# First eight taps of a per-position convolution as three products of 12-bit parts, with a scaling in PSUM

## The chip, the cores and the metric

The kernel runs on one core of a Trainium2 chip. The time is device time of one execution in microseconds (us), from the first instruction to the last, as the median of several runs. The engines that matter are TensorE (PE; its weight loads are listed apart as PEld), VectorE (DVE), ScalarE (ACT), GpSimd (POOL) and the queue that issues transfers (SP).

## What is computed

A network of four layers on x, an array of 4 images x 32 x 32 positions x 16 channels. Three layers are convolutions with weights of their own for every output position (i, j); one (the interval layer, third in order) is another small computation that shares the core. Cut to what matters, a convolution layer with M, W of 1024 x 1024 and G of 1024 x 3 x 3 x 16 x 16 is

```python
def layer(inputs, M, W, G):                       # inputs: the normalised x, (b, h, w, c)
    first = einsum('ijyx,byxc->bijc', M, inputs)
    kern = G -> (h*w*f, c, 3, 3)                  # 16 filters f for each of the 1024 output positions
    shifted = conv(inputs, kern, 'SAME')          # (b, ij, f, y, x)
    diff = relu(inputs[:, None, None] - shifted)  # (b, ij, y, x, f)
    second = einsum('ijyx,bijyxc->bijc', W, diff)
    return first - second
x = x + layer(group_norm(x), M, W, G)
```

The bulk is `shifted`: for every image, filter and output position a picture of 32 x 32, of which only a weighted sum (with W) of its clipped difference is kept. All inputs are float32.

## The kernel before

Images are worked on in two groups g of two; a phase is one group in one layer, in the order (0, layer), (1, layer) for three layers, six in all. In a phase, 8 chunks of 128 output positions are taken in turn, and in a chunk 16 filters x 2 images, so that there are 6 x 8 x 32 = 1536 steps. A step makes one PSUM tile of 128 output positions x 1024 points of the picture. The contraction is over 16 channels x 9 taps: the points' neighbourhoods lie in `im` as two halves of 64 partitions (one for the upper, one for the lower half of the picture), each with four taps x 16 channels in slots 0 and 1 (eight taps), and the ninth tap in slot 2. The two halves are separate matmuls on separate rows of TensorE, each into one bank of PSUM.

Slots 0 and 1 are plain float32 matmuls. The ninth tap goes as one matmul in the one-pass type float32r: slot 2 holds the same 16 channels four times, and `halve` with `halve_rest` changes some of the copies so that the four products are those of the high and low parts of the two factors.

VectorE then takes the minimum of the sum with 0, multiplies it with W and sums it up, in one instruction of 1024 elements per step (identity is subtracted from the weights in `prep`, so that the difference comes out of the matmul).

```python
    def halve(dst, src, mask):
        nc.scalar.activation(dst, src, AF.Copy, scale=mask[:, 1:2])

    def halve_rest(dst, src, mask):
        nc.vector.scalar_tensor_tensor(
            dst, src, mask[:, 0:1], dst.bitcast(F32), op0=ALU.mult, op1=ALU.add
        )

    def prep(u, at=0, to=FU):

        if u >= n_chunks * NU:
            return
        if at == 0:
            units[u] = (raws.pop(u), wpool.tile([P, FU, P], F32R, tag="W9", name=f"W9_{u}"))
        raw, W9 = units[u]
        f0 = u % NU * FU
        nc.gpsimd.tensor_tensor(
            raw[:, 1, at:to], raw[:, 1, at:to],
            pick[:, f0 + at : f0 + to].unsqueeze(2).to_broadcast([P, to - at, P]),
            ALU.subtract,
        )
        halve(W9[:, at:to], raw[:, 2, at:to], low_w)

    def prep_rest(u, at=0, to=FU):
        if u in units:
            raw, W9 = units[u]
            halve_rest(W9[:, at:to], raw[:, 2, at:to], low_w)
```

(cut: group norm, transposition, transfers of the neighbourhoods). The first term is a set of float32 matmuls for each group and layer, placed among the steps of a phase:

```python
    def first_term(g, layer):

        xn = xns[g]
        ps = bank(f"pf_{g}{layer}")
        for half in range(2):
            mt = wpool.tile([P, NT // 2, 4, 256], F32, tag="MT", bufs=1, name=f"MT_{g}{layer}{half}")
            nc.sync.dma_start(mt, convs[layer][0][half])
            yield 12
            for k in range(NT // 2):
                pt = NT // 2 * half + k
                for j in range(4):
                    nc.tensor.matmul(
                        ps[32 * j : 32 * j + 32, :256], lhsT=xn[:, pt, :], rhs=mt[:, k, j, :],
                        start=pt == 0, stop=pt == NT - 1, tile_position=(0, 32 * j),
                    )
        yield 2
        ft = work.tile([P, NT * GC], F32, tag="fs", name=f"ft_{g}{layer}")
        nc.vector.transpose(ft, ps[:, : NT * GC])
        yield 1
        nc.vector.tensor_tensor(
            X[g], X[g], ft.rearrange("p (t m) -> p t m", t=NT), ALU.add
        )
        yield 1
```

(cut: the interval layer, except for its inner loop.)

```python
        def step(name, ftp, rt, bias):

            ft = ivp.tile([P, QI, T1], F32, tag="ft", name=f"ft_{name}{g}")
            nc.scalar.copy(ft, ftp)
            yield 2
            s = ivp.tile([P, QI, T1], F32, tag="s", name=f"s_{name}{g}")
            last = None
            for i in range(QI + 1):
                if i < QI:
                    t = ivp.tile([P, T1, T1], F32, tag="dp", bufs=2, name=f"dp_{name}{g}{i}")
                    nc.gpsimd.tensor_tensor(
                        t,
                        ft[:, i, :].unsqueeze(1).to_broadcast([P, T1, T1]),
                        rt,
                        ALU.add,
                    )
                if last is not None:
                    nc.vector.tensor_reduce(s[:, i - 1, :], last, axis=AX.X, op=ALU.max)
                last = t
                yield 3
            for q in range(NQ):
                o = slice(GC * q, GC * (q + 1))
                nc.scalar.activation(
                    r[R:, QI * q : QI * (q + 1), :], s[o], AF.Sigmoid, bias=bias[o]
                )
            yield 2
```

The work of the next phase is a generator, `behind`: at each step's end the program resumes it if the number of steps that it last yielded have gone by. Every engine executes its instructions in the order in which the program issues them.

```python
    def conv_layer(phase, behind):

        g, layer = phases[phase]
        wait = 0
        imv = im[g].rearrange("p s b (y x) -> p s b y x", x=HP)
        im9v = im9[g].rearrange("p b (y x) -> p b y x", x=HP)
        acc = work.tile([P, NT, GC], F32, tag="acc", bufs=2, name=f"acc_{phase}")
        for t in range(NT):
            n = phase * NT + t
            steps = [(f, b) for f in range(C) for b in range(GB)]
            if n == 0:
                steps.sort(key=lambda s: (s[0] // FU, s[1]))
            for at, (f, b) in enumerate(steps):
                u = n * NU + f // FU
                if at % (FU * GB) == 2:
                    load_raw(u + 3)
                if at % (FU * GB) == (8 if u == 0 else 2):
                    prep(u + 1)
                if at % (FU * GB) == (12 if u == 0 else 8):
                    prep_rest(u + 1)
                if at == 4:
                    load_chunk(n + 1)
                W, W9 = units[u]

                ps = bank_pair(f"pc_{n}_{f}_{b}")
                for slot in range(3):
                    for h in range(2):
                        r = slice(64 * h, 64 * h + 64)
                        w, v = (W9[r], im9v[r, b]) if slot == 2 else (W[r, slot], imv[r, slot, b])
                        nc.tensor.matmul(
                            ps[:, h, :],
                            lhsT=w[:, f % FU, :],
                            rhs=v[:, :, :H],
                            start=slot == 0,
                            stop=slot == 2,
                        )

                col = b * C + f
                junk = work.tile([P, NP], F32, tag="junk", name=f"junk_{n}_{col}")
                nc.vector.scalar_tensor_tensor(
                    junk,
                    ps.rearrange("p h n -> p (h n)"),
                    0.0,
                    chunks[n],
                    op0=ALU.min,
                    op1=ALU.mult,
                    accum_out=acc[:, t, col : col + 1],
                )
                wait -= 1
                if wait <= 0:
                    wait = next(behind, 1 << 20)
            nc.vector.tensor_tensor(X[g][:, t], X[g][:, t], acc[:, t], ALU.add)
        for _ in behind:
            pass
```

The start of the program normalises the first two images itself; `normal` for the second image runs on GpSimd (three operations of 128 x 542).

## Time and profile before

| | |
|---|---|
| time, median of 3 runs | 3073.79 us (3072.03 to 3076.02) |
| span of the profiled execution | 3074.8 us |
| granted clock of TensorE | 0.999 |
| ScalarE busy | 145.8 us |
| GpSimd busy | 305.4 us |
| data moved | 215.20 MB, mean 70 GB/s |
| WT, raw: landing after issue | 6.5 us each |
| PE `pf`, line 251, x384 | 23.2 us |
| GpSimd subtraction of 128 x 1024 (line 149), mean | 1878 ns |

A row of the page's list of groups reads: line of the program, engine, operation, output<-inputs, shapes, count | busy us, mean ns of one | idle time of the engine ahead of them and what ended most of it. Busy time of PE contains the modelled tail of every matmul, so that 99% doesn't say that the array works at its peak; the distance between the starts of instructions does. The timeline has a start in us, a length in us, the engine, line, operation and count.

### The profile page before, as it was taken

What the parts mean: (1) busy time and instruction counts of PE and PEld (TensorE: products, weight loads), DVE (VectorE), ACT (ScalarE), POOL (GpSimd) and SP (SyncE); (2) the same over time, 40 slices, a digit from 0 to 9 for tenths busy, and PEclk for the clock granted to TensorE, in tenths of its full rate; (3) what the DMA queues carried; (4) which work ended last, traced back from release to release, by engine and by line L of the source; (5) the groups of instructions that cost most, each with busy time, mean ns of one, the idle gap of its engine ahead of it and who ended that gap; (6) DMA issues with size and microseconds to landing.
All of it is one profiled execution on the core that took longest, in us unless ns stands there. A gap on an engine that the chain in (4) does not pass through costs nothing.

```text
span 3074.8 us, 38073 instructions
## 1 busy us (share of the span) xinstructions
PE 3058.7 (99%) x15826; PEld 1951.4 (63%) x15826; DVE 2125.4 (69%) x3397; ACT 145.8 (5%) x156; POOL 305.4 (10%) x201
## 2 busy tenths in 40 slices
PE   8999999999999999999999999999999999999999
PEld 4555876557765556875555544685654578677776
DVE  7766666766666666666678876668877666666666
ACT  1000000000000000000000100000000000000000
POOL 3100000100000000000013310001331000000000
PEclk9999999999999999999999999999999999999999
DMA  3331112321111232111121113211113211121100
GB/s 146 125 127 67 55 49 76 102 93 48 62 62 48 72 124 76 49 63 55 48 76 49 62 63 119 76 48 53 65 48 127 76 48 71 48 76 49 69 28 2
DMA packets 36429, 215.20 MB, mean 70 GB/s; under 512 B 10400, under 2 KB 11424, under 8 KB 22560
## 3 DMA queue, kind: packets, MB, share of 16 engines
q1 hardware_dynamic: 29696, 207.65, 18.5%
q10 hardware_dynamic: 6432, 5.10, 0.8%
q8 instruction: 124, 2.03, 0.3%
q14 instruction: 49, 0.40, 0.0%
q0 software_dynamic: 128, 0.02, 0.0%
HBM read 211.77 MB, written 0.98 MB: 69 GB/s over the span
## 4 chain that ended last, share of the span: by engine, by line
PE 99%; DVE 0%; issue 0%; DMA 0%; SPq 0%; DVEq 0%
PE pc L461 98%; PE pf L251 1%; DVE junk L471 0%; DMA im<-in_xi 0%; PE ps_l L353 0%; DVE pp L315 0%; PE ps_r L369 0%; PE ps_y L422 0%; DVE im L593 0%; DVE im L601 0%; SPq L73 0%; DVE X L483 0%; DVE W L125 0%; DVEq L601 0%
## 5 line engine op out<-in xcount | busy, mean ns | idle before, releaser
L461 PE MATMUL pc<-im,raw 64*128 64x512 f32 x12288 | 2990.7, 590 | 5.4 <-DVE junk L471 3.5
L471 DVE SCALAR_TENSOR_TENSOR junk<-pc,WT 128x1024 f32<-128x1024 f32 x1536 | 1879.7, 1224 | 940.4 <-PE pc L461 934.7
L461 PEld LDWEIGHTS pc<-im,raw 64*128 64x128 f32 x12288 | 1635.8, 186 | 754.6 <-issue 461.2
L461 PE MATMUL pc<-im,W 64*128 64x512 f32 x3072 | 1636.2, 806 | 0.0
L461 PEld LDWEIGHTS pc<-im,W 64*128 64x128 f32 x3072 | 470.0, 186 | 336.4 <-issue 288.4
L149 POOL TENSOR_TENSOR raw<-raw,pick 128x1024 f32<-128x1024 f32 (+1 forms) x97 | 182.1, 1878 | 1923.9 <-DMA raw<-in_g 1824.9
L122 ACT ACTIVATE W<-raw,low_w 128x1024 fp32r<-128x1024 f32 (+1 forms) x97 | 110.6, 1141 | 2469.6 <-PE pc L461 2468.3
L125 DVE SCALAR_TENSOR_TENSOR W<-raw,low_w,W 128x1024 fp32r<-128x1024 f32 (+1 forms) x97 | 138.0, 1423 | 0.0
L471 DVE DVE_READ_ACCUMULATOR junk<-pc,WT 128x1 f32 x1536 | 127.5, 83 | 0.0
L389 POOL TENSOR_TENSOR dp_a<-ft_a,rt_r 128x1089 f32<-128x1089 f32 x16 | 39.1, 2450 | 73.2 <-DVE s_a L396 49.4
L389 POOL TENSOR_TENSOR dp_b<-ft_b,rt_r 128x1089 f32<-128x1089 f32 x16 | 37.2, 2330 | 90.1 <-DVE s_b L396 46.6
L251 PE MATMUL pf<-MT,xn 128*32 128x256 f32 x384 | 23.2, 382 | 0.0
L181 POOL PARTITION_ALL_REDUCE sum_mc<-part_mc x6 | 2.7, 445 | 190.4 <-DVE part_mc L174 184.4
L396 DVE TENSOR_REDUCE s_b<-dp_b 128x33 f32<-128x1089 f32 x16 | 20.5, 1283 | 0.0
L396 DVE TENSOR_REDUCE s_a<-dp_a 128x33 f32<-128x1089 f32 x16 | 20.5, 1282 | 0.0
L251 PEld LDWEIGHTS pf<-MT,xn 128*32 128x32 f32 x384 | 11.2, 109 | 13.1 <-issue 6.9
L483 DVE TENSOR_TENSOR X<-X,acc 128x32 f32<-128x32 f32 x48 | 11.8, 247 | 1.5
L122 ACT ACTIVATE im<-im,low_x 128x1088 fp32r<-128x1088 f32 (+1 forms) x7 | 7.5, 1073 | 110.6 <-DMA im<-xs 106.2
L181 POOL PARTITION_ALL_REDUCE sum_mi<-part_mi x2 | 0.9, 446 | 116.1 <-DVE part_mi L174 116.1
L335 DVE TENSOR_TENSOR pp<-pp 64x1024 f32<-64x1024 f32 x10 | 12.1, 1213 | 0.0
L330 DVE TENSOR_TENSOR pp<-pp 64x1024 f32<-64x1024 f32 x10 | 12.1, 1212 | 0.0
L181 POOL PARTITION_ALL_REDUCE sum_vc<-part_vc x6 | 2.6, 442 | 89.2 <-DVE part_vc L174 83.3
(96 smaller groups left out, 140.7 us busy)
## 6 DMA issues: line engine op xcount, KB each, us to landing
raw<-in_g SPq DMA_DIRECT2D x95, 1536.0 KB, 6.5
WT<-in_w SPq DMA_DIRECT2D x48, 512.0 KB, 6.5
MT<-in_mt SPq DMA_DIRECT2D x12, 2048.0 KB, 7.8
im<-xs ACTq DMA_DIRECT2D x60, 67.8 KB, 3.1
im<-xs SPq DMA_DIRECT2D x60, 67.8 KB, 3.0
im<-in_xi SPq DMA_DIRECT2D x2, 816.0 KB, 9.2
raw<-in_g SPq DMA_DIRECT2D x1, 1152.0 KB, 9.8
raw<-in_g ACTq DMA_DIRECT2D x1, 384.0 KB, 4.2
```

The costliest lines, as they stand in the source:

```text
L122: nc.scalar.activation(dst, src, AF.Copy, scale=mask[:, 1:2])
L125: nc.vector.scalar_tensor_tensor(dst, src, mask[:, 0:1], dst.bitcast(F32), op0=ALU.mult, op1=ALU.add)
L149: nc.gpsimd.tensor_tensor(raw[:, 1, at:to], raw[:, 1, at:to], pick[:, f0 + at : f0 + to].unsqueeze(2).to_broadcast([P, to - at, P]), ALU.s ...
L181: nc.gpsimd.partition_all_reduce(m, part, channels=P, reduce_op=bass_isa.ReduceOp.add)
L251: nc.tensor.matmul(ps[32 * j : 32 * j + 32, :256], lhsT=xn[:, pt, :], rhs=mt[:, k, j, :], start=pt == 0, stop=pt == NT - 1, tile_position= ...
L330: nc.vector.tensor_tensor(pp[k][:, :H, M:], a[:, :H, M:], a[:, s : H + s, M:], ALU.max)
L335: nc.vector.tensor_tensor(pp[k][:, :H, M:], a[:, :H, M:], a[:, :H, M - s : M - s + H], ALU.max)
L389: nc.gpsimd.tensor_tensor(t, ft[:, i, :].unsqueeze(1).to_broadcast([P, T1, T1]), rt, ALU.add,)
L396: nc.vector.tensor_reduce(s[:, i - 1, :], last, axis=AX.X, op=ALU.max)
L461: nc.tensor.matmul(ps[:, h, :], lhsT=w[:, f % FU, :], rhs=v[:, :, :H], start=slot == 0, stop=slot == 2,)
L471: nc.vector.scalar_tensor_tensor(junk, ps.rearrange("p h n -> p (h n)"), 0.0, chunks[n], op0=ALU.min, op1=ALU.mult, accum_out=acc[:, t, co ...
L483: nc.vector.tensor_tensor(X[g][:, t], X[g][:, t], acc[:, t], ALU.add)
```

## The change

The eight taps of slots 0 and 1 are computed from one-pass float32r matmuls. Both factors are cut into an upper part (the bits that a mask with `HIGH` leaves, 12 fewer than float32) and the lower rest; w = wu + wl and v = vu + vl. Instead of the four products wu vu, wu vl, wl vu, wl vl, the kernel forms three, with e = 2^-12:

- WU x iy = wu vu and WL x iz = wl (vl / e), summed in PSUM;
- ScalarE multiplies this sum in PSUM, in place, with 1 + e;
- WD x iyz = (wl - e wu)(vu - vl / e) is added to it by TensorE, together with the ninth tap.

Worked out, (1 + e)(wu vu + wl vl / e) + (wl - e wu)(vu - vl / e) is wu vu + wl vl / e + e wu vu + wl vl + wl vu - wl vl / e - e wu vu + wu vl, which is the whole product. The purpose is fewer passes of TensorE over the same contraction. For it

- each unit of weights now has tiles WU, WL, WD (two slots each) and W9, made by one masking on VectorE, two scalings on ScalarE, and a copy, two operations of 1024 elements and two of 512 (on 32 partitions each) on GpSimd; a unit is 4 filters instead of 8, so there are 192 units of 8 steps;
- the neighbourhoods get tiles iy, iz, iyz;
- a step has two parts: `first_part` (8 matmuls, then the scaling), and `second_part` (6 matmuls, then the sum), which is issued after the first part of the next step;
- PSUM is four pairs of banks for everything (before: three pairs and two single banks);
- the first terms of both groups are computed together, once per layer, so M is read once per layer; MT shares a buffer with the tables of the interval layer; the inner loop of that layer yields 6 steps instead of 3.

The core of the diff (cut: the start's other reorderings, buffers of the interval layer, names):

```diff
-FU = 8
+FU = 4
 NU = C // FU
 BIG = 1.0e9
+EPS = 2.0**-12
+HIGH = -(1 << 12)
 T1 = H + 1
 NQ = 4
 QI = H // NQ
...
+    def upper(src, name):
+
+        t = work.tile([P, 2, PITCH], F32, tag="upper", bufs=2, name=f"upper_{name}")
+        t = t.rearrange("p s n -> p (s n)")[:, : src.shape[1] * src.shape[2]]
+        t = t.rearrange("p (s n) -> p s n", s=src.shape[1])
+        nc.vector.tensor_scalar(
+            t.bitcast(I32), src.bitcast(I32), HIGH, None, op0=ALU.bitwise_and
+        )
+        return t
+
+    def prep(u, at=0, to=FU, eng=nc.gpsimd):
+
+        if u >= n_chunks * NU:
+            return
+        f0 = u % NU * FU
+        eng.tensor_tensor(
+            raws[u][:, 1, at:to], raws[u][:, 1, at:to],
+            pick[:, f0 + at : f0 + to].unsqueeze(2).to_broadcast([P, to - at, P]),
+            ALU.subtract,
+        )
+
+    def prep_rest(u, at=0, to=FU, eng=nc.gpsimd):
 
         if u >= n_chunks * NU:
             return
         if at == 0:
-            units[u] = (raws.pop(u), wpool.tile([P, FU, P], F32R, tag="W9", name=f"W9_{u}"))
-        raw, W9 = units[u]
-        f0 = u % NU * FU
-        nc.gpsimd.tensor_tensor(
-            raw[:, 1, at:to], raw[:, 1, at:to],
-            pick[:, f0 + at : f0 + to].unsqueeze(2).to_broadcast([P, to - at, P]),
-            ALU.subtract,
-        )
-        halve(W9[:, at:to], raw[:, 2, at:to], low_w)
-
-    def prep_rest(u, at=0, to=FU):
-        if u in units:
-            raw, W9 = units[u]
-            halve_rest(W9[:, at:to], raw[:, 2, at:to], low_w)
+            units[u] = [
+                wpool.tile([P, 2, FU, P], F32R, tag=tag, name=f"{tag}_{u}")
+                for tag in ("WU", "WL", "WD")
+            ] + [wpool.tile([P, FU, P], F32R, tag="W9", name=f"W9_{u}")]
+        src = raws[u]
+        if to == FU:
+            del raws[u]
+        w8 = src[:, :2, at:to].rearrange("p s f k -> p s (f k)")
+        w9 = src[:, 2, at:to]
+        WU, WL, WD = (t[:, :, at:to].rearrange("p s f k -> p s (f k)") for t in units[u][:3])
+        W9 = units[u][3][:, at:to]
+        high = upper(w8, f"w{u}{at}")
+        nc.scalar.activation(WD, high, AF.Copy, scale=-EPS)
+        halve(W9, w9, low_w)
+        eng.tensor_copy(WU, high)
+        eng.tensor_tensor(WL, w8, high, ALU.subtract)
+        for r in (slice(32, 64), slice(96, 128)):
+            eng.tensor_tensor(W9[r], W9.bitcast(F32)[r], w9[r], ALU.add)
+        eng.tensor_tensor(WD, WD.bitcast(F32), WL.bitcast(F32), ALU.add)
+
+    def split(eng, g, b, name):
+        high = upper(raw[:, :2, b], f"x{name}{b}")
+        eng.tensor_copy(iy[g][:, :, b], high)
+        eng.tensor_tensor(iz[g][:, :, b], raw[:, :2, b], high, ALU.subtract)
...
-                yield 3
+                yield 6
...
+    def products(ps, pairs, first):
+        for k, (w, v) in enumerate(pairs):
+            for h in range(2):
+                r = slice(64 * h, 64 * h + 64)
+                nc.tensor.matmul(
+                    ps[:, h, :],
+                    lhsT=w[r],
+                    rhs=v.rearrange("p (y x) -> p y x", x=HP)[r, :, :H],
+                    start=first and k == 0,
+                    stop=k == len(pairs) - 1,
+                    skip_group_check=not first,
+                )
+
+    def first_part(step):
+        phase, t, f, b = step
+        g = phases[phase][0]
+        n = phase * NT + t
+        WU, WL, WD, W9 = (w[..., f % FU, :] for w in units[n * NU + f // FU])
+        ps = bank_pair(f"pc_{n}_{f}_{b}")
+        products(
+            ps,
+            [(WU[:, s], iy[g][:, s, b]) for s in range(2)]
+            + [(WL[:, s], iz[g][:, s, b]) for s in range(2)],
+            True,
+        )
+        nc.scalar.activation(ps, ps, AF.Copy, scale=1.0 + EPS)
+        return ps
+
+    def second_part(step, ps):
+
+        phase, t, f, b = step
+        g = phases[phase][0]
+        n = phase * NT + t
+        WU, WL, WD, W9 = (w[..., f % FU, :] for w in units[n * NU + f // FU])
+        products(
+            ps, [(WD[:, s], iyz[g][:, s, b]) for s in range(2)] + [(W9, im9[g][:, b])], False
+        )
+        col = b * C + f
+        junk = work.tile([P, NP], F32, tag="junk", name=f"junk_{n}_{col}")
+        nc.vector.scalar_tensor_tensor(
+            junk,
+            ps.rearrange("p h n -> p (h n)"),
+            0.0,
+            chunks[n],
+            op0=ALU.min,
+            op1=ALU.mult,
+            accum_out=accs[phase][:, t, col : col + 1],
+        )
+        if (f, b) == (C - 1, GB - 1):
+            nc.vector.tensor_tensor(X[g][:, t], X[g][:, t], accs[phase][:, t], ALU.add)
+
+    accs = {}
+    open_steps = []
+
     def conv_layer(phase, behind):
 
-        g, layer = phases[phase]
+
...
-                if at % (FU * GB) == 2:
+                if at % (FU * GB) == 1:
+                    prep_rest(u + 1)
+                    prep(u + 2)
                     load_raw(u + 3)
-                if at % (FU * GB) == (8 if u == 0 else 2):
-                    prep(u + 1)
-                if at % (FU * GB) == (12 if u == 0 else 8):
-                    prep_rest(u + 1)
                 if at == 4:
                     load_chunk(n + 1)
-                W, W9 = units[u]
-
-
-                ps = bank_pair(f"pc_{n}_{f}_{b}")
-                for slot in range(3):
-                    for h in range(2):
-                        r = slice(64 * h, 64 * h + 64)
-                        w, v = (W9[r], im9v[r, b]) if slot == 2 else (W[r, slot], imv[r, slot, b])
-                        nc.tensor.matmul(
-                            ps[:, h, :],
-                            lhsT=w[:, f % FU, :],
-                            rhs=v[:, :, :H],
-                            start=slot == 0,
-                            stop=slot == 2,
-                        )
-
-                col = b * C + f
-                junk = work.tile([P, NP], F32, tag="junk", name=f"junk_{n}_{col}")
-                nc.vector.scalar_tensor_tensor(
-                    junk,
-                    ps.rearrange("p h n -> p (h n)"),
-                    0.0,
-                    chunks[n],
-                    op0=ALU.min,
-                    op1=ALU.mult,
-                    accum_out=acc[:, t, col : col + 1],
-                )
+                step = (phase, t, f, b)
+                open_steps.append((step, first_part(step)))
+                if len(open_steps) > 1:
+                    second_part(*open_steps.pop(0))
...
         def rest_of_start():
-        prep_rest(0, F0, FU)
-        for slot in (2, 0, 1):
+        for slot in (0, 1, 2):
             normal(nc.gpsimd, 1, slot)
             sides(nc.gpsimd, 1, slot)
-        yield 4
-        halve(im9[0][:, 1], im[0][:, 2, 1], low_x)
         yield 1
```

## The prediction

> **What bounds the kernel now.** I read the page from the top: busy time by engine, then the chain that ended last, then the costliest groups.

> ```profile
> PE 3058.7 (99%) x15826; PEld 1951.4 (63%) x15826; DVE 2125.4 (69%) x3397; ACT 145.8 (5%) x156; POOL 305.4 (10%) x201
> PE pc L461 98%; PE pf L251 1%; DVE junk L471 0%; DMA im<-in_xi 0%; PE ps_l L353 0%; DVE pp L315 0%; PE ps_r L369 0%; PE ps_y L422 0%; DVE im L593 0%; DVE im L601 0%; SPq L73 0%; DVE X L483 0%; DVE W L125 0%; DVEq L601 0%
> L461 PE MATMUL pc<-im,raw 64*128 64x512 f32 x12288 | 2990.7, 590 | 5.4 <-DVE junk L471 3.5
> L471 DVE SCALAR_TENSOR_TENSOR junk<-pc,WT 128x1024 f32<-128x1024 f32 x1536 | 1879.7, 1224 | 940.4 <-PE pc L461 934.7
> L122 ACT ACTIVATE W<-raw,low_w 128x1024 fp32r<-128x1024 f32 (+1 forms) x97 | 110.6, 1141 | 2469.6 <-PE pc L461 2468.3
> ```

> 98% of the chain is line 461, the products into pc. VectorE, which consumes them, waits 935 us for them; ScalarE does next to nothing. There are 1536 steps (48 chunks x 32 pairs of filter and image). Since busy matmul time is modelled, I take the cost of a pass from the distance between starts, in the timeline of the tensor rows around one step (PE, then weight loads, then VectorE; columns: start, length, engine, operation):

> ```profile
> 170.71 0.60 PE L461 MATMUL pc<-im,raw 64*128 64x512 f32 x2
> 170.74 0.81 PE L461 MATMUL pc<-im,W 64*128 64x512 f32 x2
> 171.38 0.60 PE L461 MATMUL pc<-im,raw 64*128 64x512 f32 x2
> 171.14 0.44 PEld L461 LDWEIGHTS pc<-im,raw 64*128 64x128 f32 x4 [0.23 <-DVE junk L471]
> 171.59 1.23 DVE L471 SCALAR_TENSOR_TENSOR junk<-pc,WT 128x1024 f32<-128x1024 f32 x1 [0.72 <-PE pc L461]
> ```

> "x2" is the two row halves, which run side by side. Each full f32 product is split in two instructions (12288 / 1536 = 8 in a step = 2 taps' slots x 2 halves x 2). From the last f32 instruction (170.71) to the load issued when the f32r pass (W) begins (171.14) is 0.43 us; from there to the next f32 start (171.38) is 0.24 us. A step is 4 x 0.43 + 0.24 = 1.96 us, and the sums of VectorE indeed start every 1.963 us (1499.43, 1501.40, 1503.36 in the timeline). 1536 x 1.963 = 3015 us; the other 59 us are the start (10), the first terms (23, line 251), the interval layer and small holes.

> So an f32 slot is four plain passes of 0.215 us, and an f32r slot is one pass that took 0.24. That last 0.03 matters, because the new kernel consists of such passes.

> [...] in the trace two products of 110 columns with 64x128 loads between them start 0.10 us apart (1649.11 and 1649.21), so loads should not hold up passes of 0.215, and I don't know what the 0.03 is. [...]

> **The change part by part.**

> *Removed from TensorE:* the two f32 slots (8 passes). *Added:* six f32r slots (upper x upper, lower x lower, third product, two each). With the ninth tap that is 7 passes for 9. The pass is between 0.215 (half of 0.43) and 0.243; I choose 0.225. If nothing else held it up, a step would be 7 x 0.225 = 1.575 us, or 2419 us for 1536.

> *Added to ScalarE, every step:* a scaling of 128x1024 in PSUM. The copies of line 372 out of PSUM take 258, 364 and 474 ns for 110, 231 and 352 elements, so about 0.16 + 0.89 ns per element = 1.07 us. TensorE does the first part of step k+1 (4 passes) and the second part of step k-1 (3 passes) meanwhile, 1.575 us, so by itself the scaling is hidden: 0.2 (drain) + 1.07 + 0.16 = 1.43.

> *VectorE:* the sum of 1.15 us to the next start (the accumulator read begins 1.15 after it) stays; halve_rest (138 us) goes; one masking of 1024 words comes per unit. A tensor_scalar of 542 elements took 558 ns, one of 256 took 353; [...] I take U = 0.75. About 11 us per unit of 8 steps: not the bound.

> *GpSimd, per unit of 4 filters:* subtraction of 128x512 (1.0, half of the row at line 149), a copy (about 1.5), two 1024-element operations (1.9 each), two 512-element ones (1.0 each): 8.3 us of some 15. It has its time unless the interval layer's 2.4 us additions come in its way.

> *What lies on the path: the order on ScalarE.* At step 1 of each unit the program puts prep_rest ahead of first_part. ScalarE executes in program order, so it gets the scaling of WD and the halving of W9 for the next unit before scaling k. The scaling of WD waits for the mask on VectorE, and this is queued behind the sum of step k-2. Counting from the end of first part k-1, with pass p:
> - second part k-2: 3p; drain until the sum starts 0.20 (171.59 - 171.385); sum 1.15; mask U; signal 0.05;
> - WD 1.06 less 0.09 overlap = 0.96 (rounded down); half of the 256- and 768-element rows of line 122 (497, 938) for W9 = 0.72, less overlap 0.63; scaling 1.07;
> - signal and first load 0.16 (0.05 + 0.10, a matmul after an idle row half took 0.69 in place of 0.59).
> Sum: 3p + 4.22 + U. Without it, TensorE would come to second part k after 3p + 4p + 3p + 4p = 14p. It stands still for 4.22 + U - 11p = 4.97 - 2.475 = 2.5 us once a unit. The next scaling isn't late, but TensorE can't catch up, since it is the bound. A unit is 8 x 7p + 2.5 = 15.1 us; 192 units make 2898 us.

> *The rest:* 59 us as before (the first terms keep their matmuls, in three lumps; half of the 24 MB of MT traffic goes, which was hidden), plus about 15 at the start (the second image is needed after 4 steps instead of 8, and GpSimd normalises it in three operations of 2.2 us, ahead of unit 1's preparation), plus about 20 where VectorE waits for the interval layer's additions behind preparation. 2898 + 94 = 2992; I say 2990.

> **The rivals.**
> 1. *TensorE stays the bound and the ScalarE order costs nothing.* For it: the steady step has a margin of 0.15 us and ScalarE is idle 95% now. Against it: program order, as above. 2419 + 80 = 2500 us.
> 2. *f32r passes take 0.243 each in a row.* For it: the only f32r pass in the trace takes that. Against it: the only one stands between f32 passes, and could pay for the transition. The unit is 45p + 4.22 + U = 15.9 us: 3053 + 94 = 3147[...]. With p = 0.215 it is 2812 + 94 = 2906.
> 3. *GpSimd becomes the bound* if copies or additions to f32r run at the 4 ns per element of line 601's 542 elements in 2.2 us. Then its unit takes some 15 us or more, and the time is 3000 to 3200.
> 4. *The clock falls:* a stop of 2.5 us in every 15 brings holes that the kernel before hasn't. Its granted clock was 0.999. At half clock for a few us of each unit, 3300.

> **Range and chances.** The two pass costs lie at 2906 and 3147, almost equally likely to me, and straddle the 2% line at 3012; the mask and GpSimd only add; the first rival subtracts a lot but I give it one in eight. Prediction 2990 us, range 2780 to 3190; faster by over 2%: 0.52, within 2%: 0.23, slower: 0.25.

> **What would show it.** Pass: the distance of f32r starts within one part, 0.215 or 0.243. Stop: once in 8 steps a gap of about 2.5 us in PE, and in the waits a total of some 480 us of TensorE for ScalarE's pc; ScalarE's own wait for the mask some 300. Scaling: row of pc<-pc on ACT near 1.07 us. [...] GpSimd: about 1600 us busy. VectorE: 70 to 75% busy. The prediction is wrong if the gap is absent (then near 2500) or if a wait for GpSimd's W tiles appears in every unit.

## The result, and the profile after

The changed kernel takes **3542.53 us** (3539.26 to 3547.17, four runs) where the kernel before takes 3074.90: a ratio of **1.1523, 95% interval 1.1503 to 1.1543**. It is slower by 468 us, and it lies 550 us above the predicted 2990, outside the range of 2780 to 3190.

From the page of the changed kernel: busy times, granted clock in 40 slices, then groups of instructions (busy us, mean ns of one | idle time ahead of them and what ended it).

```profile
PE 2966.8 (84%) x21970; PEld 2346.7 (66%) x21970; DVE 2155.1 (61%) x3519; ACT 1874.1 (53%) x1993; POOL 1983.0 (56%) x1284
PEclk8899999899999989999988899898889989999999
L531 ACT ACTIVATE pc<-pc 128x1024 f32<-128x1024 f32 x1536 | 1527.9, 1002 | 1174.3 <-PE pc L510 1128.0
L510 PE MATMUL pc<-iyz,WD 64*128 64x512 f32 x6144 | 1134.6, 442 | 531.4 <-ACT pc L531 519.1
L200 POOL TENSOR_TENSOR WL<-raw,upper_w 128x1024 fp32r<-128x1024 f32 (+1 forms) x192 | 456.6, 2378 | 115.1 <-PE pc L510 57.2
L203 POOL TENSOR_TENSOR WD<-WD,WL 128x1024 fp32r<-128x1024 f32 (+1 forms) x192 | 460.0, 2396 | 15.0
L197 ACT ACTIVATE WD<-upper_w 128x1024 fp32r<-128x1024 f32 (+1 forms) x193 | 203.2, 1053 | 395.4 <-DVE upper_w L164 384.2
L164 DVE TENSOR_SCALAR upper_w<-raw 128x1024 int32<-128x1024 int32 (+1 forms) x193 | 139.4, 722 | 19.7 <-POOL raw L174 19.3
```

TensorE still is the engine with the most work, but its second products wait 519 us for the scaling of line 531 (before, all idle time ahead of its products was 5 us). ScalarE, which should be free for it, waits 384 us for the mask of line 164 ahead of the scaling of WD (line 197). The granted clock is 0.911 on average (0.999 before), and the digit falls below 9 in slices all over the run.

The stop of one unit is in the timelines of ScalarE and of VectorE (start, length, engine, line, operation, count [idle time ahead of it]):

```profile
1001.33 1.01 ACT L531 ACTIVATE pc<-pc 128x1024 f32<-128x1024 f32 x1 [0.71 <-PE pc L510]
1004.05 1.06 ACT L197 ACTIVATE WD<-upper_w 128x1024 fp32r<-128x1024 f32 x1 [1.72 <-DVE upper_w L164]
1005.01 0.71 ACT L142 ACTIVATE W<-raw,low_w 128x512 fp32r<-128x512 f32 x1
1005.63 1.91 ACT L531 ACTIVATE pc<-pc 128x1024 f32<-128x1024 f32 x2
```

```profile
1002.12 1.23 DVE L545 SCALAR_TENSOR_TENSOR junk<-pc,WT 128x1024 f32<-128x1024 f32 x1 [0.47 <-PE pc L510]
1003.27 0.69 DVE L164 TENSOR_SCALAR upper_w<-raw 128x1024 int32<-128x1024 int32 x1
```

VectorE's sum ends at 1003.27, then the mask runs; ScalarE stands until 1004.05, does the scaling of WD and the halving of W9, and only at 1005.63 comes to the scaling of PSUM that TensorE needs. TensorE's own timeline shows what this costs ("x4" is two passes, each as two row halves side by side; "x2" is one pass):

```profile
1003.49 0.74 PE L510 MATMUL pc<-iy,WU 64*128 64x512 f32 x4
1003.98 0.74 PE L510 MATMUL pc<-iz,WL 64*128 64x512 f32 x4
1006.68 1.02 PE L510 MATMUL pc<-iyz,WD 64*128 64x512 f32 x4 [1.96 <-ACT pc L531]
1007.50 0.63 PE L510 MATMUL pc<-im,W 64*128 64x512 f32 x2
1007.92 1.06 PE L510 MATMUL pc<-iy,WU 64*128 64x512 f32 x4
1008.78 1.06 PE L510 MATMUL pc<-iz,WL 64*128 64x512 f32 x4
1009.63 0.98 PE L510 MATMUL pc<-iyz,WD 64*128 64x512 f32 x4
1010.45 0.41 PE L510 MATMUL pc<-im,W 64*128 64x512 f32 x2
1010.69 0.65 PE L510 MATMUL pc<-iy,WU 64*128 64x512 f32 x4
1011.18 0.65 PE L510 MATMUL pc<-iz,WL 64*128 64x512 f32 x4
```

Two passes take 0.49 us (1003.49 to 1003.98, and again 1010.69 to 1011.18). The pair at 1003.98 was followed not at 1004.47 but at 1006.68: the stop is 2.2 us. After it the same pairs take 0.86 and 0.85 (1007.92, 1008.78, 1009.63), until 1010.45. The 9 passes from 1006.68 to 1010.45 take 3.77 us in place of 9 x 0.2436 = 2.19 (0.2436 is the mean of a pass in undisturbed steps, those in which nothing waits), so this slow stretch costs 1.58 us on top of the stop. With it a unit is 56 x 0.2436 = 13.64, + 2.2 + 1.58 = 17.42, the median distance of units in the trace.

But not every stop is followed by a slow stretch. Two units earlier the stop is as long (2.15 us), and the passes behind it are at 0.49 at once:

```profile
970.53 0.65 PE L510 MATMUL pc<-iz,WL 64*128 64x512 f32 x4
973.17 0.75 PE L510 MATMUL pc<-iyz,WD 64*128 64x512 f32 x4 [1.99 <-ACT pc L531]
974.00 0.65 PE L510 MATMUL pc<-iy,WU 64*128 64x512 f32 x4
974.49 0.65 PE L510 MATMUL pc<-iz,WL 64*128 64x512 f32 x4
```

The difference is where the stop lies. In the traces of this case the granted clock changes only on a fixed grid of 3.413 us: all 884 changes in the twelve of them fit such a grid, each trace its own, to 0.6 ns. In windows of this grid around the two stops (window, length, TensorE's busy time and count, granted clock, share and rate of DMA):

```profile
969.41:972.82 3.41, 1.77 (x16) 1.00 0.01 2
972.82:976.24 3.42, 3.07 (x26) 1.00 0.00 0
1003.55:1006.96 3.41, 1.45 (x12) 1.00 0.00 0
1006.96:1010.37 3.41, 3.41 (x18) 0.50 0.00 0
```

The first stop (971.02 to 973.17) falls into two windows, 1.80 and 0.35 us; the second (1004.47 to 1006.68) lies whole in one, and the next window is at half clock. Over all twelve traces, with idle time counted as what two starts lie apart beyond one pass: of 9257 windows at full clock with under 1.8 us idle none was followed by half clock, of 58 with 1.8 to 2.0 us 16 were, and of 420 with more 414. In the changed kernel 47 of the 192 units have no half clock in them, and their median is 16.1 us. Where nothing else disturbs the units, it is as a rule one in four: 3 x 17.4 + 16.1 = 68.3 us, which is 20 windows.

So the way from before to after can be laid out. Before: 1536 steps of 1.963 us, 3015, and 59 of rest. The slow clock's share is what all passes at half clock take beyond 0.2436 us each.

| | us |
|---|---|
| before | 3075 |
| passes: a step from 1.963 to 7 x 0.2436 = 1.705 us, x 1536 | -396 |
| the stop, 2.2 us x 192 units | +422 |
| passes at half clock, summed over the run | +234 |
| everything else: 263 in place of 59 | +204 |
| after | 3539 |

### The profile page after: what moved, and what is told of

The parts are those of the page before. It is cut to its first block, busy times and chain, and to the rows that moved or that the text cites. A ratio compares the mean times of both kernels' runs of the same rounds, so it can differ in the third digit from the quotient of the medians.

```text
span 3538.9 us, 56292 instructions
## 1 busy us (share of the span) xinstructions
PE 2966.8 (84%) x21970; PEld 2346.7 (66%) x21970; DVE 2155.1 (61%) x3519; ACT 1874.1 (53%) x1993; POOL 1983.0 (56%) x1284
## 4 chain that ended last, share of the span: by engine, by line
PE 73%; ACT 9%; issue 6%; POOL 5%; DVE 4%; DMA 2%; ACTq 0%; DVEq 0%; POOLq 0%; SPq 0%
PE pc L510 73%; ACT pc L531 5%; ACT W L142 4%; DVE junk L545 2%; POOL W L202 1%; DMA raw<-xs 1%; POOL WD L203 1%; POOL WL L200 1%; DVE upper_w L164 1%; PE pf L318 1%; POOL raw L174 0%; DMA xs<-xt 0%; POOL tables L384 0%; POOL raw L702 0%; POOL WU L199 0%
## 5 line engine op out<-in xcount | busy, mean ns | idle before, releaser
L531 ACT ACTIVATE pc<-pc 128x1024 f32<-128x1024 f32 x1536 | 1527.9, 1002 | 1174.3 <-PE pc L510 1128.0
L510 PE MATMUL pc<-iyz,WD 64*128 64x512 f32 x6144 | 1134.6, 442 | 531.4 <-ACT pc L531 519.1
L510 PEld LDWEIGHTS pc<-iyz,WD 64*128 64x128 f32 x6144 | 657.1, 206 | 755.8 <-ACT pc L531 558.5
L510 PE MATMUL pc<-iy,WU 64*128 64x512 f32 x6144 | 1103.1, 431 | 18.3 <-DVE junk L545 10.0
L510 PE MATMUL pc<-iz,WL 64*128 64x512 f32 x6144 | 1096.2, 428 | 8.5 <-POOL WL L200 7.3
L510 PEld LDWEIGHTS pc<-iy,WU 64*128 64x128 f32 x6144 | 676.9, 205 | 178.1 <-DVE junk L545 14.8
L510 PEld LDWEIGHTS pc<-iz,WL 64*128 64x128 f32 x6144 | 677.0, 203 | 153.8 <-POOL WL L200 9.3
L510 PE MATMUL pc<-im,W 64*128 64x512 f32 x3072 | 695.9, 433 | 0.0
L200 POOL TENSOR_TENSOR WL<-raw,upper_w 128x1024 fp32r<-128x1024 f32 (+1 forms) x192 | 456.6, 2378 | 115.1 <-PE pc L510 57.2
L202 POOL TENSOR_TENSOR W<-W,raw 32x512 fp32r<-32x512 f32 (+1 forms) x384 | 490.8, 1278 | 26.4
L203 POOL TENSOR_TENSOR WD<-WD,WL 128x1024 fp32r<-128x1024 f32 (+1 forms) x192 | 460.0, 2396 | 15.0
```

Of the source, the lines that this page charges most:

```text
L200: eng.tensor_tensor(WL, w8, high, ALU.subtract)
L202: eng.tensor_tensor(W9[r], W9.bitcast(F32)[r], w9[r], ALU.add)
L203: eng.tensor_tensor(WD, WD.bitcast(F32), WL.bitcast(F32), ALU.add)
L510: nc.tensor.matmul(ps[:, h, :], lhsT=w[r], rhs=v.rearrange("p (y x) -> p y x", x=HP)[r, :, :H], start=first and k == 0, stop=k == len(pair ...
L531: nc.scalar.activation(ps, ps, AF.Copy, scale=1.0 + EPS)
```

## The experiments

Three questions: is the slow stretch really a consequence of the stop, and the stop of the order on ScalarE; what stands in the rest; and why an f32r pass takes 0.244 where an f32 pass before took 0.215 (half of the 0.43 from one f32 instruction's start to the next). All kernels start from the changed one.

### Filling the stop with useless products

```diff
-        products(ps, [...first part...], True)
+        for _ in range(times):                     # 3 at step 2 of each unit, else 1
+            products(ps, [...first part...], True)
```

The first part of one step per unit is done three times over, each restarting the sum: 8 passes more, nothing new in the result.

> At step 2 of every unit the first part's four passes are issued three times in place of once (the last one counts), so 8 passes of 0.243 us = 1.94 us of useless matmuls lie in the stop of about 2.4 us. Theory (the stop lets the granted clock fall, and the slow passes after it cost about 1.4 us a unit): granted clock back to 0.99 or more, a unit from 17.4 to about 16.0 us, time about 3275 us, with more work done. Rival (the clock has another cause, or the slow passes cost nothing on the path): the clock stays near 0.91 and the time is 3540 us or more, up to 3540 + 192 x 1.94 = 3910.

Measured: **3392.07 us** (ratio to before 1.1031, interval 1.1009 to 1.1053). TensorE has 1528 passes more to do (8 in each unit but the last), and the kernel is 150 us faster than the changed one; the granted clock rises from 0.911 to 0.973. One whole unit of it, first the stop in TensorE's timeline, then the table for the 16 us:

```profile
950.82 0.65 PE L510 MATMUL pc<-iz,WL 64*128 64x512 f32 x4
951.70 0.75 PE L510 MATMUL pc<-iyz,WD 64*128 64x512 f32 x4 [0.24 <-ACT pc L532]
952.29 0.40 PE L510 MATMUL pc<-im,W 64*128 64x512 f32 x2
952.53 0.65 PE L510 MATMUL pc<-iy,WU 64*128 64x512 f32 x4
```

```profile
950.00:966.00 16.00, 15.76 (x130) 12.00 (x128) 10.40 (x18) 9.58 (x11) 9.39 (x7) 1.00 0.21 76
```

The undisturbed unit is 16.0 us: 64 passes of 0.2436 are 15.6, and a stop of 0.4 is left (951.70 where 951.31 was due). The clock stays at 1.00 through it. So the stop cost more than its own length: with 1.95 us of useless work in its 2.2 us a unit is as short as those that had met no half clock (16.1), and 1.4 us shorter than the others. The gain is less than the expected 265 us, and the clock doesn't reach 0.99: what passes lose at half clock falls from 234 to 54 us, and of these 180 us 150 arrive in the time. Where the other 30 go was not told apart.

### The mask one step earlier

```diff
+                if at % (FU * GB) == 0 and u + 1 < n_chunks * NU:
+                    early = upper(raws[u + 1][:, :2]..., f"w{u + 1}0")
                 ...
-                    prep_rest(u + 1)
+                    prep_rest(u + 1, high=early)
```

The order on ScalarE stays; only what its first instruction waits for is there sooner.

> Only the mask on VectorE is issued one step earlier (step 0 of a unit); the order on ScalarE stays. Theory (the stop is made of ScalarE's wait for the mask plus its own two operations ahead of scaling k): ScalarE no longer waits, the two operations alone put scaling k back, stop about 0.5 us, too short for the clock to fall; unit 13.6 + 0.5 = 14.1 us, time about 192 x 14.1 + 194 = 2900 us. Rival (the stop comes from GpSimd's preparation or from PSUM): the stop stays near 2.4 us and the time near 3540 us.

Measured: **3096.68 us** (ratio 1.007, 1.005 to 1.0091), 446 us faster than the changed kernel by the place of one instruction on VectorE. Lines of its waits (engine, line, waited for: us in total, times, longest), and of TensorE's timeline:

```profile
PE pc L511 <- ACT pc L532: 223.2, 203, 8.6
ACT WD L198 <- DVE upper_w L164: 81.0, 41, 5.1
```

```profile
1000.39 0.65 PE L511 MATMUL pc<-iz,WL 64*128 64x512 f32 x4
1001.30 0.76 PE L511 MATMUL pc<-iyz,WD 64*128 64x512 f32 x4 [0.25 <-ACT pc L532]
1001.89 0.41 PE L511 MATMUL pc<-im,W 64*128 64x512 f32 x2
1002.14 0.66 PE L511 MATMUL pc<-iy,WU 64*128 64x512 f32 x4
1002.63 0.66 PE L511 MATMUL pc<-iz,WL 64*128 64x512 f32 x4
```

ScalarE's wait for the mask falls from 384 to 81 us. The stop is 0.4 us now (1001.30 where 1000.88 was due), and the passes after it are at full speed at once (0.49 for two). The undisturbed unit is 14.28, near the expected 14.1. The time is 197 us above the expected 2900 all the same: the median unit is 14.59, which makes 94 us, and the rest (the span less 192 median units) is 289 us where 194 were allowed.

### The scaling of WD behind the scaling of PSUM

```diff
+    def prep_parts(u, ...):                        # in place of prep_rest
         high = upper(w8, f"w{u}{at}")
-        nc.scalar.activation(WD, high, AF.Copy, scale=-EPS)
-        halve(W9, w9, low_w)
         eng.tensor_copy(WU, high)
         eng.tensor_tensor(WL, w8, high, ALU.subtract)
+        yield                                      # after the scaling of step 2
+        nc.scalar.activation(WD, high, AF.Copy, scale=-EPS)
+        yield                                      # after the scaling of step 3
+        halve(W9, w9, low_w)
         (the additions to WD and W9; then prep and load of the units after)
```

> The two ScalarE operations for the next unit are issued behind the scalings of steps 2 and 3, when the mask is long done. Theory: no stop, granted clock 0.99, unit 8 x 7 x 0.243 = 13.6 us, time about 192 x 13.6 + 194 = 2810 us, 8 to 9% faster than the kernel before. Rival (ScalarE has too little room: 8 x 1.0 + 1.05 + 0.7 = 9.8 us in 13.6, and every scaling is needed within 1.7 us): smaller stops at steps 3 and 4 remain, 2900 to 3000 us.

Measured: **3011.90 us** (ratio 0.9796, 0.978 to 0.9813). Undisturbed units take 13.64 us, which is 56 x 0.2436: no stop is left in them, and this order alone is worth 531 us. But the expected time was some 200 below, and the rival's range ends below 3012 too. The median unit is 13.76, and 3010.5 - 192 x 13.76 leaves 368 us of rest. Units more than 2 us above the median hold 352 of these; they lie in the first units of the phases, where the group norm for the next phase is done, and in the two phases during which the interval layer is done. GpSimd's timeline in one of them:

```profile
1041.94 2.38 POOL L198 TENSOR_TENSOR WL<-raw,upper_w 128x1024 fp32r<-128x1024 f32 x1
1050.24 0.44 POOL L246 PARTITION_ALL_REDUCE sum_vc<-part_vc  x1 [5.91 <-PE pc L516]
1058.33 2.33 POOL L203 TENSOR_TENSOR WD<-WD,WL 128x1024 fp32r<-128x1024 f32 x1 [7.65 <-issue]
1060.74 2.59 POOL L205 TENSOR_TENSOR W<-W,raw 32x512 fp32r<-32x512 f32 x2
```

and in TensorE's:

```profile
1060.71 1.22 PE L516 MATMUL pc<-iyz,WD 64*128 64x512 f32 x4 [6.12 <-POOL WD L203]
```

The group norm's sum over partitions is listed with 0.44 us, yet GpSimd executes nothing else between 1044.3 and 1058.3: 5.91 us ahead of it and 7.65 behind it, the latter put down to "issue", that is to nothing that the profile shows. Behind this stands the addition that completes WD, and TensorE waits 6.12 us for that. All 16 sums of this trace stand so: 5.9 to 7.8 us of idle time ahead, and 6.9 to 7.65 behind (behind eight of them with one copy in between). In the changed kernel it is 5.7 to 6.2 ahead and, behind the copy that follows each, 6.7 to 7.8: these make up the 115.1 us of idle time in its row of line 200. The kernel before has the same 16 sums on GpSimd, with holes of 6.8 to 7.5 us ahead of the next subtraction behind them in its trace, but there GpSimd had, apart from the interval layer, one operation of 1.9 us in a unit of 31 us, and nobody waited.

### The group norm's sums on TensorE

```diff
-            m = work.tile([P, GC // 2], F32, tag="sum", ...)
-            nc.gpsimd.partition_all_reduce(m, part, channels=P, reduce_op=bass_isa.ReduceOp.add)
+            m = bank(f"sum_{name}")[:, : GC // 2]
+            nc.tensor.matmul(m, lhsT=ones, rhs=part, start=True, stop=True)
```

and the two pauses behind these sums in the schedule go from 5 steps to 1.

> As e3, with the 8 all-reduces of the group norms taken from GpSimd and done by a matmul with a matrix of ones. Theory (an all-reduce holds GpSimd for some 14 us, 6 ahead of it and 7.7 behind it in the trace of e3, the preparation of the next unit stands behind it, and TensorE waits some 10 us at each): 8 x 10 to 8 x 14 us less, plus what follows from them, 2850 to 2930 us. Rival (the holes at the phases' starts come from VectorE's group norm and from the splitting on GpSimd): within 1% of e3, 2980 to 3040 us.

Measured: **2875.36 us** (ratio 0.9348, 0.9332 to 0.9363), 137 us less than the kernel before it in this chain. The median unit is the same 13.76; the rest is 233 in place of 368. That is 8.5 us for each of the 16 sums, where the timeline showed GpSimd held for some 14 us by one, so not all of it was on the path. How much of the 137 is the shorter pauses' share was not tried apart.

### What an f32r pass costs

Three kernels from the third one (the order repaired, sums still on GpSimd), each executed once. Each changes one thing that could make the pass 0.244.

**Neighbouring elements.** The products read 512 elements in a row; what is left out is the step over the two border columns of each picture row, so that the points are not those of the reference.

```diff
-                    rhs=v.rearrange("p (y x) -> p y x", x=HP)[r, :, :H],
+                    rhs=v[r, : NP // 2],
```

> As e3, but every product reads 512 neighbouring elements in place of 16 rows of 32 at a pitch of 34 (it leaves out the step over the two border columns, so its values are others). Theory A (an f32r pass of 0.243 instead of 0.216 comes from reading rows that don't lie side by side): passes of 0.216, step 1.51 us, time about 300 us below e3, near 2510. Theory B (it is in the type or in the weight loads): passes of 0.243 and the time of e3.

Measured: 2911.07 us, passes of about 0.231, step 1.615. A gain of 0.013 a pass, half of what was to be explained.

**Two-byte parts.** `F32R` becomes bfloat16 for the parts of weights and neighbourhoods, rows of 32 as before; the values are coarser than the method needs.

> As e3, with bfloat16 in place of float32r for the weight parts and the neighbourhood parts (half the bytes of every operand; the parts lose bits, so the values are coarser). Theory A (the surcharge of an f32r pass comes from reading 4-byte rows of 32 that don't lie side by side): passes of 0.216 us, step about 1.51 us, time 2720 to 2820 us. Rival (any operand read in rows of 32 pays it, or the weight loads do): passes of 0.243, time of e3, 3012 us.

Measured: 2792.21 us, step 1.511.

**Half columns.** Each matmul is cut in two of 256 columns, with twice the weight loads:

```diff
+                for c in range(2):
+                    nc.tensor.matmul(ps[:, h, 256 * c : 256 * c + 256], ...,
+                        rhs=v.rearrange("p (y x) -> p y x", x=HP)[r, 8 * c : 8 * c + 8, :H], ...)
```

> As e3, with every matmul cut in two of 256 columns (8 rows each), the same elements in all and twice the weight loads. If the surcharge of 0.028 us goes with the rows read: two halves cost 0.243 together, time of e3, 3012 us within 1%. If it is paid per matmul (start or load of weights): 2 x (0.107 + 0.028) = 0.27, step 1.88 us, about 3280 us.

Measured: 3056.10 us, between the two expectations and near the first; step 1.754 (the uncut one 1.705). TensorE's timelines, first of the kernel with two-byte parts, then of that with half columns, side by side with the 0.49 of two passes above:

```profile
902.85 0.61 PE L516 MATMUL pc<-iy,WU 64*128 64x512 bf16 x4
903.28 0.61 PE L516 MATMUL pc<-iz,WL 64*128 64x512 bf16 x4
```

```profile
902.31 0.68 PE L517 MATMUL pc<-iy,WU 64*128 64x256 f32 x8
902.81 0.69 PE L517 MATMUL pc<-iz,WL 64*128 64x256 f32 x8
903.32 0.68 PE L517 MATMUL pc<-iyz,WD 64*128 64x256 f32 x8
```

With two bytes an element, two passes take 0.43 us, 0.216 each, with the same rows, the same count of matmuls and of weight loads. With twice as many matmuls and loads, two passes' worth takes 0.50 to 0.51: the doubling adds about 0.007 a pass, not a second 0.029. So the surcharge is not one per matmul or per weight load; it goes with reading four-byte operands, and with the layout they are read in. Both operands became two-byte at once, so which one counts was not told apart.

### Both repairs together: dense rows

The neighbourhoods iy, iz, iyz and the ninth tap's are written without the border columns, so that the products read 512 neighbouring elements and still the right points. From the kernel with the sums on TensorE:

```diff
-    iy = [const.tile([P, 2, GB, PITCH], F32R, ...)]            # iz, iyz, im9 alike
+    iy = [const.tile([P, 2, GB, NP // 2], F32R, ...)]
-        eng.tensor_copy(iy[g][:, :, b], high)
+        eng.tensor_copy(packed(iy[g][:, :, b]), cropped(high))
-                    rhs=v.rearrange("p (y x) -> p y x", x=HP)[r, :, :H],
+                    rhs=v[r],
```

> As e7, and the parts of the neighbourhoods are written side by side (rows of 32 at a pitch of 32), so that every product reads 512 neighbouring elements and the result is the whole one. From e4, whose passes took 0.230: step 1.61 us, 100 us below e7, 2750 to 2830 us. If packing costs VectorE, GpSimd or ScalarE more than it brings TensorE: the time of e7 or more.

Measured: **2766.86 us** (ratio **0.8997, 0.8984 to 0.901**): the fastest of all, 10% faster than before and 22% faster than the changed kernel, with the change's whole arithmetic. Two passes take 0.47 or 0.46 us in its timeline:

```profile
902.13 0.63 PE L524 MATMUL pc<-iy,WU 64*128 64x512 f32 x4
902.60 0.63 PE L524 MATMUL pc<-iz,WL 64*128 64x512 f32 x4
903.06 0.63 PE L524 MATMUL pc<-iyz,WD 64*128 64x512 f32 x4
```

### Which layouts are dear

From dense rows to rows at pitch 34 a pass goes from 0.2325 to 0.2445, a step of 5% (means of all passes under 0.3 us in the dense kernel and the one before it; 0.2324 and 0.2436 by their steps of 1.627 and 1.705). Two more kernels from the dense one, each executed once, test whether every break between rows costs this, whatever its length (theory B), with the reading `[r, :, :H]` from rows of other pitches. The first has iy at pitch 36, iz dense, iyz at 33, the ninth tap at 40:

```diff
-    iy  = ... [P, 2, GB, NP // 2]      iyz = ... [P, 2, GB, NP // 2]      im9 = ... [P, GB, NP // 2]
+    iy  = ... [P, 2, GB, 16 * 36]      iyz = ... [P, 2, GB, 16 * 33]      im9 = ... [P, GB, 16 * 40]
```

> The best version so far (dense tiles, 2767 us, passes 0.2325 us on average) with the row pitch of the neighbourhoods changed tile by tile: iy rows of 32 at pitch 36, iz dense, iyz at pitch 33, the ninth tap's at 40. The whole result is computed. Open: why rows of 32 at pitch 34 cost 0.2445 a pass and dense ones 0.2325. [...] Theory B (every break between rows costs, whatever its length): iy, iyz and ninth tap 0.2445, iz 0.2325; step about 1.69, time about 2865.

Measured: 2780.70 us, step 1.642. Mean distance from a pass to the next, by the tile that it streams: pitch 40 0.232, dense 0.232, pitch 36 0.2345, pitch 33 0.238. The second has all four at pitch 33:

> The best version so far with all neighbourhoods in rows of 32 at pitch 33, whole result. [...] Theory B (every break costs the same): 0.2445 as at pitch 34, step 1.71, time about 2890.

Measured: 2799.79 us, step 1.654, passes 0.237 on average. Theory B is wrong here: the break between rows costs nothing at pitch 40, 0.002 at 36 and 0.005 to 0.006 at 33, where 34 costs 0.012. What remains is that pitch 34 is the dearest of the five tried (0.2445) and that pitches 40 and 36 are as good as dense or nearly so (0.232 and 0.2345 for 0.232). Why 33 beats 34 (0.237 for 0.2445), and why even dense f32r takes 0.2325 and not bf16's 0.216, stays open.

## Why the prediction was wrong, step by step

**The order on ScalarE: right, in mechanism and in size.** The prediction's formula for the stop, 4.22 + U - 11p, gives 2.26 us with the measured mask (0.722) and pass (0.2436); measured 2.2. ScalarE keeps the program's order in the trace: the scaling of WD, the halving of W9 and the scaling of PSUM follow one another so in all 192 units. Neighbours there overlap by a median of 0.094 (1004.05 + 1.06 reaches past 1005.01), for the 0.09 in the formula. From the scaling's end to the matmul that waits for it the median is 0.054, for 0.05; from the mask's end to the scaling of WD 0.093, for an estimated 0.05. Foreseen were waits of 480 (TensorE for ScalarE) and 300 (ScalarE for the mask); they are 519 and 384. The scaling took 1.00 for 1.07, that of WD 1.05 for 1.06, the mask 0.72 for an estimated 0.75.

**The pass: the term mis-sized.** "I choose 0.225", the middle between 0.215 and 0.243; it is 0.2436. The only f32r pass in the trace of before had shown 0.24, and the argument against it (it might pay for a transition) was a guess. It adds 56 x 0.0186 = 1.04 us a unit, 200 us; the shorter stop takes 0.3 of it back, some 55 us.

**The clock: the step that failed.** The prediction's sum charges a stop with its own length alone. It held the clock as rival 4, one of several alternatives, though the sum itself contained a 2.5 us stop in every 15. It isn't an alternative but a consequence of the stop: filled, it left the clock at 1.00. It added 234 us in all. The pass at its measured cost and the stop together make 3137, still inside the range; the clock takes the time out of it. At a granted clock of 0.50 two passes took 0.86 for 0.49, and the windows are 3.413 us long. Some 2 us idle in one of them were enough for half clock in the next (414 of 420 with more than 2.0). Stops of 0.4 us were not, nor a stop of 2.15 us that two windows share.

**The rest: 263 in place of 94.** The start was right: the first sum begins at 26.6 us (before 14.0), 13 us later where 15 were allowed. Not seen was that the group norm's sums hold GpSimd, now an engine with work that others wait for. GpSimd's own work per unit is 9.5 us for the estimated 8.3 (the operations of 1024 elements 2.38 and 2.40 for 1.9, those of 512 on 32 partitions 1.28 for 1.0, the copy 1.04 for 1.5), and it was busy 1983 us for 1600. It is not the bound that rival 3 feared. Once the stop was gone, taking the sums off GpSimd was worth 137 us; how much of the changed kernel's own 263 they are was not measured apart.

Summed: 2992 + 200 - 55 + 234 + 169 = 3540, against a span of 3539. Rival 2 (pass of 0.243, 3147) and rival 4 were both true, and they add; the range had treated them as exclusive. Rival 4 had about the right size (310 us over 2990, measured 234), though half clock came in three units of four and not in each.

## What to carry to other kernels

When a change inserts a stop of a few microseconds into a stream of matmuls, count the slow passes behind it in the same sum: here 2.2 us of stop cost 3.8 in three units of four. Before moving work to an engine that was idle, put its queue down in program order, with what the first instruction in it waits for, and look for long operations that nobody waited for until now. A cheaper type is worth its count of passes only at its own measured pass time: 7 f32r passes for 9 f32 passes' worth saved 13% of TensorE's step in rows of pitch 34 and 17% (1.627 us) in dense ones, not 22%.
